# Two layers over 64 graphs on one core: attention rows divided before they are turned, and outputs in seven half-size products

## The chip, the core and the metric

The kernel runs on one core of a Trainium2 chip. The metric is device time in microseconds (us) from the first to the last instruction of an execution with what lies around it, as the median of several runs. A profiled execution has a time of its own, and its trace covers a span that is a little shorter. The engines are named as in the profile: PE (matmuls), PEld (its weight loads), DVE (VectorE), ACT (ScalarE), POOL (GpSimd) and SP (which here only issues DMAs).

## The reference

Everything is float32. There are 64 graphs of 256 nodes with 512 features each.

```python
# layer 0: x is (64, 256, 512), adj is (64, 256, 256)
h = relu(layernorm(x))
q = h @ Wq.T + bq;  k = h @ Wk.T + bk;  v = h @ Wv.T + bv
w = adj * exp(q @ k.T)
w = w / w.sum(axis=2, keepdims=True)
x = x + w @ v
# layer 1
h = relu(layernorm(x))
A = adj + I;  d = A.sum(-1) ** -0.5
x = x + (A * d[:, :, None] * d[:, None, :]) @ (h @ W1 + b1)
```

## The kernel before

Two graphs make a pair, and there are 32 pairs. The products with Wq and Wk are merged once, at the start, into one matrix, so that each pair has six stages of matmuls:

- **g** (`pm_g`): the merged matrix times the features, which gives "keys" that already hold both projections;
- **v** (`pm_v`): the values;
- **s** (`pm_s`): the scores, written with keys on the partitions and queries along the row, so that the exponentials `wT` are already turned for the next product;
- **o** (`pm_o`, line 545): weights times values;
- **l** (`pm_l`): adjacency times normed features of layer 1;
- **w** (`pm_w`): the result of l times W1.

All but o are written as block products of half-size matrices by the Strassen-Winograd scheme: seven half-size products in place of eight, with sums of blocks before (the operands called S and T) and after. One product accumulates into a PSUM bank called the chain (product 1, then 6, 7 and 4), one into a bank called rest (5, then 3), and product 2 into a bank called side. Between two products into the chain somebody has to read the bank: most often ACT copies it (tags A0, A1, U2, U3, or the tile yS in l). The stages g, v and w have 28 matmuls of 256 columns, s and l 28 of 128. A float32 matmul shows as two instructions in the profile, so 28 matmuls are 56 records.

The stage o is plain. For each of four blocks of 128 queries and each half of the 512 features it multiplies twice, over two blocks of keys, and an extra column of ones beside the values gives the row sum: 16 matmuls, 32 records. DVE takes the reciprocal of the sum (L553) and adds the scaled product to x (L555).

Other work that is named later:

- `move_quadrants` (L311): DVE turns the features in 32x32 blocks, and then ACT copies 16 strips per pair to their places in `hT`.
- `normed` (L267): ACT's layer norm with relu, four instructions per layer and pair; the statistics are L250 and L251 on DVE, followed by five small operations on POOL.
- In l and w (`convolution`), ACT copies the product l7 (L695), scales w's first product by d (L662) and copies the product l4 into b21, a part of the tile yS (L702); DVE adds (L697), and POOL makes further sums.
- L593 adds the graph bias on DVE, and L452 writes a block of the values.
- L815 and L603 to L607 prepare the adjacency on POOL.

The kernel is written with a library that puts each engine's instructions into a queue at compile time, by when they come ready in its own reckoning, and that sets the waits. `tc.issue_after(ins)` keeps instructions behind one on the same engine. The helper `in_order` keeps most matmuls in the order of the text (in s and o they are free), and other work is hung behind named readers:

```python
work = {
    "key P1": [(measure_and_weigh, p)],
    "key P6": [(second_norm, p - 1), (find_node_sums, p - 1)],
    "key C21": [(norm_features, p + 1)],
    "key C12": [(turn_blocks, p + 1), (find_key_sums, p)],
    "value P6": [(move, p + 1, 0, 4)],
    "value C11": [(find_terms, p + 1)],
}
```

In l and w of the kernel before, the order of products is l7, w1, l4, l3, w2, then the other five of w.

Of the kernel before, what the change touches and what calls it, by code (L numbers as in the profile page):

```python
# [16 lines left out]
def kernel(  # L17
# [33 lines left out]

    nc = tc.nc
    P = 128
# [15 lines left out]
    xp = ctx.enter_context(tc.tile_pool(name="xp", bufs=3))  # L69
# [7 lines left out]
    x_tiles, a_tiles, q_tiles = {}, {}, {}  # L77

# [6 lines left out]
    def load_x(p):  # L85
        x_tiles[p] = xp.tile([P, TB, D], F32, tag="x", name=f"x_{p}")
        for g in range(G):
            nc.sync.dma_start(of_graph(x_tiles[p], g), in_dram(x, p, g))

    def load_a(p):  # L90
        a_tiles[p] = ap.tile([P, TB, N], F32, tag="a", name=f"a_{p}")
        for g in range(G):
            nc.sync.dma_start(of_graph(a_tiles[p], g), in_dram(adj, p, g))
        if p == 0:
            return


        q_tiles[p] = p1.tile([P, NB, G * N // Q, Q], F32, tag="aq", name=f"aq_{p}")
        blocks = adj[G * p : G * p + G].rearrange(
            "g (j c) (kt i r) -> i c kt (g j) r", c=Q, i=NQ, r=Q  # L100
        )
        for i in range(NQ):
            nc.sync.dma_start(q_tiles[p][i * Q : (i + 1) * Q], blocks[i])
# [6 lines left out]
    w1_21 = const.tile([P, 2, HD], F32, tag="w1_21", name="w1_21")  # L110
# [13 lines left out]
    load_x(0)  # L124
    load_a(0)
    nc.sync.dma_start(wv_rows, wv.rearrange("(c p) d -> p c d", p=P))
    load_x(1)
# [6 lines left out]
    nc.sync.dma_start(b1_all, b1.partition_broadcast(P))  # L134

# [7 lines left out]
    v = const.tile([P, TB, D + 1], F32, tag="v", name="v")  # L143
    nc.gpsimd.memset(v[:, :, HD : HD + 1], 1.0)

# [6 lines left out]
    sub, add, mult = ALU.subtract, ALU.add, ALU.mult  # L152
# [17 lines left out]
    def merge_query_key():  # L170
        m21 = p1.tile([P, 2, HD], F32, tag="A1", name="m21")
        for half, dcs in ((0, (0, 1)), (1, (0, 1)), (0, (2, 3)), (1, (2, 3))):
            for dc in dcs:
                pm = ps_m.tile([P, HD], F32, tag="pm", name=f"pm_mT_{dc}_{half}")
                for oc in range(DC):
                    nc.tensor.matmul(  # L176
                        pm,
                        wk_rows[:, oc, ts(dc, P)],
                        wq_rows[:, oc, ts(half, HD)],
# [17 lines left out]
    def bias_products():  # L197
# [4 lines left out]
        g_rows, last = weighted_rows(wq_rows, bkT, "A0")  # L202
# [13 lines left out]
    def key_row(c_rows):  # L216
        pc = ps_m.tile([P, D], F32, tag="pm", name="pc_c")
        nc.tensor.matmul(pc, ones_sq, c_rows, start=True, stop=True)
        nc.scalar.copy(c_all, pc)
# [14 lines left out]
    last_sums = {}  # L234

    def inverse_root(src, plus, name):
# [3 lines left out]
        r = sm.tile([P, TB], F32, tag="ir_r", name=f"irr_{name}")  # L240
# [3 lines left out]
    def scale_offset(p, name, scale=None):  # L244

        xt = x_tiles[p]
        mv = sm.tile([P, TB, 2], F32, tag="mv", name=f"mv_{name}")
        for t in range(TB):
            st = sm.tile([P, 6], F32, tag="st", name=f"st_{name}_{t}")
            nc.vector.bn_stats(st, xt[:, t, :])  # L250
            last_sums[name] = nc.vector.bn_aggr(mv[:, t, :], st).ins  # L251
# [11 lines left out]
    def normed(p, name, rd, nb):  # L263

        h = p2.tile([P, TB, D], F32, tag="h", name=f"h_{name}")
        for t in range(TB):
            nc.scalar.activation(  # L267
                h[:, t, :],
                x_tiles[p][:, t, :],
# [4 lines left out]
        return h  # L274

    def key_terms(p, h):

        acc = sm.tile([P, TB], F32, tag="ka", name=f"ka_{p}")
        scratch = p1.tile([P, D], F32, tag="U3", name=f"hc_{p}")
        for t in range(TB):  # L280
            nc.vector.scalar_tensor_tensor(  # L281
                scratch, h[:, t, :], 1.0, c_all, mult, mult, accum_out=acc[:, t : t + 1]
            )
        ks = sm.tile([P, TB], F32, tag="ks", name=f"ks_{p}")
        nc.vector.tensor_scalar(ks, acc, s0[:, 0:1], None, add)
        return ks

    def blocks_transposed(p, h):

        hq = p1.tile([P, TB, D], F32, tag="hq", name=f"hq_{p}")  # L290
        for t in range(TB):
            nc.vector.transpose(hq[:, t, :], h[:, t, :])
        return hq

    def transposed_features(p, h):

        hT = p2.tile([P, DC, NT], F32, tag="hT", name=f"hT_{p}")
        for t in range(TB):
            pt = ps_m.tile([P, DC, P], F32, tag="pm", name=f"pt_h_{p}_{t}")
            for dc in range(DC):  # L300
                nc.tensor.transpose(pt[:, dc, :], h[:, t, ts(dc, P)], ident)  # L301
            nc.scalar.copy(hT[:, :, ts(t, P)], pt)
        return hT

    def move_quadrants(hq, hT, which):

        src = hq.rearrange("p t (dc j c) -> p j dc t c", j=NQ, c=Q)
        dst = hT.rearrange("p dc (t i c) -> p i dc t c", i=NQ, c=Q)
        for n in which:
            i, j = n // NQ, n % NQ  # L310
            last = nc.scalar.copy(dst[j * Q : (j + 1) * Q, i], src[i * Q : (i + 1) * Q, j])  # L311
        return last.ins

    def feature_sums(p, hT):

        b11, b12 = hT[:, 0:2, 0:N], hT[:, 0:2, N:NT]
        b21, b22 = hT[:, 2:4, 0:N], hT[:, 2:4, N:NT]
        hS = p2.tile([P, 3, 2, N], F32, tag="hS", name=f"hS_{p}")
        t1, t2, t4 = (hS[:, i] for i in range(3))
        eng = nc.vector if p == 0 else nc.gpsimd  # L320
        eng.tensor_tensor(t1, b12, b11, sub)
        eng.tensor_tensor(t2, b22, t1, sub)

        eng.tensor_tensor(b12, b22, b12, sub)
        eng.tensor_tensor(t4, b21, t2, sub)
        return (b11, b21, b22, t1, t2, b12, t4)

    def key_sums(p, gT):

        a11, a21 = gT[:, 0:2, 0:N], gT[:, 0:2, N:NT]  # L330
        a12, a22 = gT[:, 2:4, 0:N], gT[:, 2:4, N:NT]
        gS = p1.tile([P, 3, 2, N], F32, tag="gS", name=f"gS_{p}")
        s1, s2, s4 = (gS[:, i] for i in range(3))
        eng = nc.vector
        eng.tensor_tensor(s1, a21, a22, add)
        eng.tensor_tensor(s2, s1, a11, sub)

        eng.tensor_tensor(a21, a11, a21, sub)
        eng.tensor_tensor(s4, a12, s2, sub)
        return (a11, a12, a22, s1, s2, a21, s4)  # L340

    last_product = [None]

    def in_order(*args, **kwargs):

        with tc.issue_after(last_product[0]) if last_product[0] else ExitStack():
            last_product[0] = nc.tensor.matmul(*args, **kwargs).ins  # L347

    def products_of(name, w, weight_moves):

        banks = {}

        def product(bank, which, part, start):

            if start:
                banks[bank] = ps_m.tile([P, 2, HD], F32, tag="pm", name=f"pm_{name}_{bank}")
            for r in range(2):  # L360
                for dt in range(2):
                    left, right = w[:, which, dt, :], part[:, dt, :]
                    if weight_moves:
                        left, right = right, left
                    in_order(
                        banks[bank][:, r, :],
                        left[:, ts(r, P)],
                        right,
                        start=start and r == 0 and dt == 0,
                        stop=r == 1 and dt == 1,  # L370
                        skip_group_check=True,
                    )
            return banks[bank]

        return product

    def temp(tag, name):
        return p1.tile([P, 2, HD], F32, tag=tag, name=f"{tag}_{name}")

    def projections(p, parts, then, fill_first, fill_second):  # L380

        b11, b21, b22, t1, t2, t3, t4 = parts
        gT = p1.tile([P, DC, NT], F32, tag="gT", name=f"gT_{p}")
        keys_of = products_of(f"g_{p}", m_set, False)  # L390
        values_of = products_of(f"v_{p}", v_set, True)

        def bias(i, r):
            return gb[:, 2 * i + r : 2 * i + r + 1]

        def key_block(i, g):
            return gT[:, 2 * i : 2 * i + 2, ts(g, N)]

        def key_sum(i, g, pm, more):
            for r in range(2):  # L400
                last = nc.vector.scalar_tensor_tensor(  # L401
                    key_block(i, g)[:, r, :], pm[:, r, :], bias(i, r), more[:, r, :], add, add
                )
            return last

        def value_block(i, g):
            return v[:, 2 * g : 2 * g + 2, i * (HD + 1) : i * (HD + 1) + HD]

        def behind(ins, place):
            with tc.issue_after(ins.ins):  # L410
                then(place)

        a, u2, u3 = (temp(tag, f"g{p}") for tag in ("A1", "U2", "U3"))
        chain = keys_of(0, A11, b11, True)
        behind(nc.scalar.copy(a, chain), "key P1")  # L415
        rest = keys_of(2, S1, t1, True)
        keys_of(0, S2, t2, False)
        behind(nc.scalar.copy(u2, chain), "key P6")
        side = keys_of(1, A12, b21, True)
        behind(key_sum(0, 0, side, a), "key C11")  # L420
        keys_of(0, S3, t3, False)
        behind(nc.scalar.copy(u3, chain), "key P7")
        behind(key_sum(1, 1, rest, u3), "key C22")
# [528 lines left out]
```

## Time and profile before

| | |
|---|---|
| median of 3 runs | 1825.99 us (1825.42 to 1826.48) |
| profiled execution, own time | 1824.66 us |
| its span | 1822.9 us |
| PE / PEld / DVE / ACT / POOL busy | 99% / 90% / 70% / 47% / 51% |
| granted clock of PE | 1.0 throughout |
| DMA | 148.44 MB, 81 GB/s over the span |

Busy time is the time in which an engine has an instruction under way. PE's matmuls are pipelined and their ends are modelled, so its 99% does not say by itself that it is at its peak. A row of the groups gives line, engine, operation, tiles, shape and count, then total busy time and the mean of one in ns, and then idle time just before and who ended it. Where instructions of an engine overlap, busy time divided by the count is less than the mean of one. A row of a timeline gives start, duration, engine, line, operation and tiles, and in brackets the idle time before it and who ended that.

### The profile page before, as it was taken

Reading aid. Unit: us, or ns where it says so; the run is one execution under the profiler, and the core shown is the slowest. Engines: PE = TensorE matmul, PEld = TensorE weight load, DVE = VectorE, ACT = ScalarE, POOL = GpSimd, SP = SyncE. Lnnn points to the kernel's source line nnn. Section 1 sums busy time; section 2 is a strip of 40 time slices with the busy share of each in tenths; the row PEclk is TensorE's granted clock in tenths of the full one; section 3 lists DMA queues with packets and bytes.
Section 4 is the critical chain, followed back from the end, with each engine's and each line's share of the span. In section 5 each row is a group of like instructions: output and inputs, shape, how many; then the busy total and the mean of one; then the engine's idle time right before and its main releaser. Section 6 shows DMA issues by size and latency. Waiting matters only on the chain.

```text
span 1822.9 us, 28081 instructions
## 1 busy us (share of the span) xinstructions
PE 1810.8 (99%) x10114; PEld 1639.7 (90%) x10114; DVE 1267.9 (70%) x3030; ACT 861.3 (47%) x1604; POOL 927.5 (51%) x1099
## 2 busy tenths in 40 slices
PE   9999999999999999999999999999999999999998
PEld 8899989999999999899999999998999999999987
DVE  7867677676677676776766776767767677667664
ACT  4544554444544445544455444455444554444522
POOL 2564444655445644446554456444465544564435
PEclk9999999999999999999999999999999999999999
DMA  9444235433345342354342444423444334534111
GB/s 231 69 89 93 55 62 99 90 90 84 43 89 99 85 95 51 66 99 88 92 82 42 93 99 86 94 51 66 99 89 91 82 41 93 99 86 94 31 24 47
DMA packets 224267, 148.44 MB, mean 81 GB/s; under 512 B 150272, under 2 KB 170752, under 8 KB 224128
## 3 DMA queue, kind: packets, MB, share of 16 engines
q1 hardware_dynamic: 206112, 112.03, 28.7%
q0 software_dynamic: 16960, 33.56, 11.0%
q8 instruction: 81, 1.33, 0.4%
q10 hardware_dynamic: 1056, 1.05, 0.2%
q14 instruction: 58, 0.48, 0.1%
HBM read 112.99 MB, written 33.62 MB: 80 GB/s over the span
## 4 chain that ended last, share of the span: by engine, by line
PE 98%; POOL 1%; DVE 1%; issue 0%; ACT 0%; DVEq 0%; POOLq 0%; ACTq 0%
PE pm_g L347 21%; PE pm_v L347 21%; PE pm_w L347 21%; PE pm_o L545 12%; PE pm_s L490 11%; PE pm_l L347 11%; PE pm_mT L176 1%; PE pm_run_in L168 0%; ACT h_b L267 0%; DVE hc L281 0%; POOL x L674 0%; DVE x L668 0%; PE pt_h L301 0%; DVE ad L576 0%; PE pt_wv L226 0%
## 5 line engine op out<-in xcount | busy, mean ns | idle before, releaser
L347 PE MATMUL pm_w<-w_set,yS 128*128 128x256 f32 x1792 | 399.2, 380 | 3.2 <-DVE x L668 2.0
L347 PEld LDWEIGHTS pm_w<-w_set,yS 128*128 128x128 f32 x1792 | 335.4, 190 | 46.7 <-DVE x L668 2.6
L311 ACT COPY hT<-hq 32x512 f32<-32x512 f32 x496 | 305.4, 616 | 6.6
L698 POOL TENSOR_TENSOR yS<-yS,U_l 128x512 f32<-128x512 f32 x32 | 40.6, 1268 | 479.9 <-DVE yS L697 479.9
L347 PE MATMUL pm_v<-v_set,hT 128*128 128x256 f32 x1024 | 236.8, 379 | 0.0
L347 PE MATMUL pm_g<-hT,m_set 128*128 128x256 f32 x1024 | 236.7, 379 | 0.0
L668 DVE SCALAR_TENSOR_TENSOR x<-pm_w,irr_d,x 128x256 f32<-128x256 f32 x256 | 111.9, 479 | 166.7 <-PE pm_w L347 145.7
L545 PE MATMUL pm_o<-v,wT 128*128 128x257 f32 (+1 forms) x1024 | 227.3, 379 | 0.0
L347 PEld LDWEIGHTS pm_g<-hT,m_set 128*128 128x128 f32 x1024 | 194.7, 190 | 26.8 <-issue 0.5
L545 PEld LDWEIGHTS pm_o<-v,wT 128*128 128x128 f32 x1024 | 191.3, 189 | 26.6 <-DVE wT L511 0.3
L347 PEld LDWEIGHTS pm_v<-v_set,hT 128*128 128x128 f32 x1024 | 192.4, 190 | 24.8
L347 PE MATMUL pm_v<-v_set,hS 128*128 128x256 f32 x768 | 176.5, 380 | 0.0
L347 PE MATMUL pm_g<-hS,m_set 128*128 128x256 f32 x768 | 176.2, 379 | 0.0
L347 PEld LDWEIGHTS pm_g<-hS,m_set 128*128 128x128 f32 x768 | 146.0, 190 | 19.8
L401 DVE SCALAR_TENSOR_TENSOR gT<-pm_g,gb,U_g 128x256 f32<-128x256 f32 x128 | 56.1, 479 | 152.8 <-PE pm_g L347 111.1
L347 PEld LDWEIGHTS pm_v<-v_set,hS 128*128 128x128 f32 x768 | 143.5, 190 | 18.2
L674 POOL TENSOR_TENSOR x<-x,U_w 128x512 f32<-128x512 f32 x64 | 81.3, 1270 | 102.4 <-ACT U_w L662 99.7
L415 ACT COPY A_g<-pm_g 128x512 f32<-128x512 f32 x32 | 18.7, 585 | 235.2 <-PE pm_g L347 234.4
L555 DVE SCALAR_TENSOR_TENSOR x<-pm_o,rsum,x 128x256 f32<-128x256 f32 x256 | 110.4, 473 | 1.1
L815 POOL TENSOR_TENSOR aT<-aT,ident 128x128 f32<-128x128 f32 x128 | 65.8, 560 | 72.1 <-DVE wT L511 72.1
L347 PE MATMUL pm_l<-aT,h_b 128*128 128x128 f32 x768 | 96.3, 275 | 0.5 <-DVE U_l L689 0.5
L490 PE MATMUL pm_s<-hT,gT 128*128 128x128 f32 x768 | 96.4, 275 | 0.2
(153 smaller groups left out, 3187.4 us busy)
## 6 DMA issues: line engine op xcount, KB each, us to landing
x<-in_x_dram SPq DMA_DIRECT2D x64, 512.0 KB, 4.8
x<-in_L_gnn_Wv_b_dram POOLq DMA_DIRECT2D x32, 1024.0 KB, 11.0
out_dram<-x SPq DMA_DIRECT2D x62, 512.0 KB, 3.4
a<-in_adj_dram SPq DMA_DIRECT2D x64, 256.0 KB, 11.6
aq<-in_adj_dram SPq DMA_DIRECT2D x124, 128.0 KB, 4.4
drow<-dflat SPq DMA_DIRECT2D x32, 256.0 KB, 4.5
wq_rows<-in_L_gnn_Wq_w_dram ACTq DMA_DIRECT2D x2, 512.0 KB, 7.6
wk_rows<-in_L_gnn_Wk_w_dram SPq DMA_DIRECT2D x2, 512.0 KB, 6.8
```

Source lines behind the costliest of these rows:

```text
L176: nc.tensor.matmul(pm, wk_rows[:, oc, ts(dc, P)], wq_rows[:, oc, ts(half, HD)], start=oc == 0, stop=oc == DC - 1,)
L311: last = nc.scalar.copy(dst[j * Q : (j + 1) * Q, i], src[i * Q : (i + 1) * Q, j])
L347: last_product[0] = nc.tensor.matmul(*args, **kwargs).ins
L401: last = nc.vector.scalar_tensor_tensor(key_block(i, g)[:, r, :], pm[:, r, :], bias(i, r), more[:, r, :], add, add)
L415: behind(nc.scalar.copy(a, chain), "key P1")
L490: nc.tensor.matmul(banks[bank][:, g, :], left[:, dt, ts(g, P)], right[:, dt, ts(g, P)], start=start and g == 0 and dt == 0, stop=g == 1 an ...
L545: nc.tensor.matmul(pm[:, 0:width], wT[:, kb, qb, g, :], v[:, kb * G + g, lo : lo + width], start=kb == 0, stop=kb == NB - 1,)
L555: nc.vector.scalar_tensor_tensor(xh, pm[:, 0:HD], rsum, xh, mult, add)
L668: last = nc.vector.scalar_tensor_tensor(to, pm[:, r, :], factor(nb, r), to, mult, add)
L674: return nc.gpsimd.tensor_tensor(block(i, nb), block(i, nb), more, add)
L698: nc.gpsimd.tensor_tensor(t2, b22, part, sub)
L815: last = nc.gpsimd.tensor_tensor(diag, diag, ident, add)
```

## The change

- The roles of query and key in the merged matrix are exchanged, so that the scores stand with queries on the partitions (`e`), and the mask gives the row sums by its accumulator.
- `scale_weights` divides the rows on ACT, `turn_weights` turns them in 32x32 blocks on DVE, and `move_weights` copies 16 strips to their places in `wT` on ACT.
- The stage o becomes a seven-product scheme with sums of weights and of values on POOL, and three of its results go to x by way of ACT and POOL.
- The value tile loses its columns of ones. The features are loaded a second time into a tile of their own, in which they are normed in place; x is then loaded later into two buffers in place of three.
- All matmuls of the stages follow one list of tokens: a letter for the stage, a number for the product (1 to 7). Work hangs behind the readers of a token. In the round of pair p, the letters g, v and s belong to pair p+1, and o, l and w to pair p.

The core of the diff:

```diff
+    def scale_weights(p):
+        rs = sm.tile([P, TB], F32, tag="rsum", name=f"rsum_{p}")
+        nc.vector.reciprocal(rs, row_sums[p])
+        for t in range(TB):
+            row = weights[p][:, t // G, t % G]
+            nc.scalar.mul(row, row, rs[:, t : t + 1])
+
+    def turn_weights(p):
+        turned[p] = p1.tile([P, NB, G, NB, P], F32, tag="gS", name=f"eq_{p}")
+        for qb in range(NB):
+            nc.vector.transpose(
...
+    def move_weights(p, first, last):
+        if first == 0:
+            wTs[p] = p1.tile([P, NB, G, NB, P], F32, tag="wT", name=f"wT_{p}")
+        src = turned[p].rearrange("p qb g kb (j c) -> p j (qb g kb) c", c=Q)
+        dst = wTs[p].rearrange("p qb g kb (i c) -> p i (qb g kb) c", c=Q)
+        for n in range(first, last):
+            i, j = n // NQ, n % NQ
+            nc.scalar.copy(dst[j * Q : (j + 1) * Q, i], src[i * Q : (i + 1) * Q, j])
+
+    def find_weight_sums(p):
...
+        weight_parts[p] = left_sums(nc.gpsimd, quarters, wS)
+
+    def find_value_sums(p):
...
+        eng = nc.gpsimd if p < NP - 1 else nc.vector
+        value_parts[p] = right_sums(eng, quarters, vS)
...
-        for qb in range(NB):
-            for g in range(G):
-                t = qb * G + g
-                rsum = sm.tile([P, 1], F32, tag="rsum", name=f"rsum_{p}_{t}")
-                for half in range(2):
-                    width = HD + 1 - half
-                    lo = half * (HD + 1)
-                    pm = ps_m.tile([P, HD + 1], F32, tag="pm", name=f"pm_o_{p}_{t}_{half}")
-                    for kb in range(NB):
-                        nc.tensor.matmul(
...
-                    if half == 0:
-                        nc.vector.reciprocal(rsum, pm[:, HD : HD + 1])
-                    xh = xt[:, t, ts(half, HD)]
-                    nc.vector.scalar_tensor_tensor(xh, pm[:, 0:HD], rsum, xh, mult, add)
+    def output_stage(p):
...
+        def into(n, i, bank):
+            read(nc.vector.tensor_tensor(block(n, i), bank, block(n, i), add))
+
+        def by_way_of(tag, n, i):
+            more = temp(tag, f"o{p}")
+            read(nc.scalar.copy(more, pm["chain"]))
+            read(nc.gpsimd.tensor_tensor(block(n, i), block(n, i), more, add))
+
+        def p_1():
+            pm["chain"] = product(0, a11, b11, True)
+            by_way_of("A0", 0, 0)
...
+    def value_stage(p):
...
+        def p_7():
+            product(0, t3, S3)
+            u3 = temp("A1", f"v{p}")
+            read(nc.scalar.copy(u3, pm["chain"]))
+            read(nc.vector.tensor_tensor(block(1, 1), pm["rest"], u3, add))
+
+        def p_4():
+            product(0, t4, A22)
+            read(nc.vector.tensor_copy(block(1, 0), pm["chain"]))
...
+    def neighbour_stages(p):
...
+        def l_4():
+            gather(0, a22, u4)
+            read(nc.scalar.copy(b21, pm["l"]))
...
+        def w_2():
+            into(0, 0, product(1, b21, A12, True))
...
+    def run(order, stages, work=None):
...
+            begun[letter][number]()
+            todo = [c for c in (work or {}).get(token, ()) if c[1] < NP]
+            if todo:
+                with ExitStack() as behind:
+                    for ins in last_read.values():
+                        behind.enter_context(tc.issue_after(ins))
+                    for call, p, *more in todo:
+                        call(p, *more)
...
+    def work_around(p):
...
+            "g1": [(turn_adjacency, p), (norm_features, p + 2)],
+            "g6": [(find_weight_sums, p)],
...
+            "o3": [(measure_again, p)],
+            "v5": [(find_query_sums, p + 1)],
+            "v6": [(move, p + 2, 12, 16), (second_norm, p), (find_node_sums, p), (load_features, p + 3)],
+            "s1": [(find_terms, p + 2)],
+            "s3": [(load_a, p + 3)],
+            "l7": [(scale_weights, p + 1)],
+            "l3": [(find_feature_sums, p + 2)],
+            "w2": [(turn_weights, p + 1)],
+            "w6": [(move_weights, p + 1, 0, 6)],
+            "w5": [(measure, p + 3)],
+            "w7": [(move_weights, p + 1, 6, 16)],
+            "w3": [(find_value_sums, p + 1)],
+            "w4": [(add_graph_bias, p), (store, p), (load_x, p + 2)],
...
+    for p in range(NP - 2):
+        run(
+            "g1 g5 g6 g2 g7 o1 o5 g4 o6 g3 o2 o7 v1 o4 o3 v5 v6 v2 v7 s1 s6 v4 s5 v3 s7 "
+            "l1 s2 l2 s4 l6 s3 l5 l7 w1 l4 l3 w2 w6 w5 w7 w3 w4",
+            around(p),
+            work_around(p),
+        )
```

The work behind o6, o7 and v1 includes the other 12 strips of the features of pair p+2 (four, two and six). `read` notes an instruction as the last reader on its engine. The list above serves 30 pairs; the first pair has a list of its own, and so have the last two, in which the weights of the last pair are scaled behind s3 and moved behind v6 and v2.

## The prediction, made before the changed kernel was run

> **What bounds the kernel now.** I read the page's shares first, then its chain, then the long form of the chain, then one pair's window.
>
> ```profile
> PE 1810.8 (99%) x10114; PEld 1639.7 (90%) x10114; DVE 1267.9 (70%) x3030; ACT 861.3 (47%) x1604; POOL 927.5 (51%) x1099
> PE 98%; POOL 1%; DVE 1%; issue 0%; ACT 0%; DVEq 0%; POOLq 0%; ACTq 0%
> ```
>
> A busy share of PE alone proves little, but the chain that ended last is 98% PE: nearly every matmul waited only for the one before it. The chain in order of time repeats itself:
>
> ```profile
> 1620.42 6.93 PE pm_o L545 x32
> ...
> 1659.50 10.41 PE pm_w L347 x48
> 1669.91 6.25 PE pm_s L490 x56
> 1676.16 6.93 PE pm_o L545 x32
> ```
>
> One pair of graphs takes 1676.16 - 1620.42 = 55.74 us. A 256-column matmul instruction (a matmul is two records) costs 6.93/32 = 0.2166 us for o and 10.41/48 = 0.2169 for w; g's row 8.63/40 gives 0.2158. A 128-column one costs 6.25/56 = 0.1116. Three stages of 56 at 0.2158, two of 56 at 0.1116 and o's 32 make 36.3 + 12.5 + 6.9 = 55.7: the period is issue of matmuls and nothing else. The table of stretches agrees (columns: window, its length, then busy PE, PEld, DVE, ACT, POOL):
>
> ```profile
> 1340.00:1395.74 55.74, 55.74 (x315) 50.55 (x314) 39.09 (x94) 26.97 (x51) 28.75 (x34) 1.00 0.44 81
> ```
>
> So fewer matmuls pay one for one, and so does every wait that PE gains.
>
> [...] two of L815 took 0.88 us, and 1.18 us beside DVE's masks.
>
> **The change, part by part.**
>
> *Matmuls.* o falls from 32 instructions to 7 products x 2 graphs x 2 = 28: 6.93 - 28 x 0.2158 = 0.89 us per pair, 28.4 us in 32 pairs. The first pair's adjacency is no longer turned on PE (26.08 to 26.95 in PE's timeline): 0.9. Together **-29.3 us**. Scores by query and the new order change no count. The period would be 54.85.
>
> *Added load, per pair.* ACT: 16 pieces of the turned weights; the operation is not in the trace. Each has 256 elements per partition, so between the 0.372 of a 128x256 copy and L311's 0.616; [...] 6.4 us. Four scalings of 128x256: 0.419 each from L662 (53.6/128), at most 0.47 by interpolation in the other activations; I take 0.45: 1.8. Three copies at 0.585: 1.8. ACT goes from 27.0 to 37. POOL: three additions at 1.27, four weight sums at about 0.74 (as L603 to L607), four value sums at 1.27: 11.9, so 28.8 to 40.7. DVE: two transposes (1.3) and accumulating masks (2.0) replace masks (1.6), reciprocals (0.7) and L555 (3.5, against four 128x512 additions, 2.8): 39.1 to about 39.5. All fit under 54.85 as totals, so PE covers them unless a single wait sticks out. The second load of x adds 1 MB per pair to DMA engines busy 44%; it is issued a pair ahead and hidden. SP issues two more loads per pair, and at a pair's end the next x waits behind the store in the same buffer; POOL's addition of bv into it comes 16 us of matmuls later, against some 3.4 for a store and 4.8 for a load. Cost zero; if a load came late, POOL would hold o's sums and the second norm.
>
> *Wait A: the division in front of b21.* The list puts `scale_weights` behind l7; after it come w1, l4, l3, w2. w2 needs b21, which ACT copies from l4. The kernel before has the same four steps in the same order:
>
> ```profile
> 1377.12 1.89 PE L347 MATMUL pm_w<-w_set,yS 128*128 128x256 f32 x8
> 1377.36 0.58 ACT L695 COPY A_l<-pm_l 128x512 f32<-128x512 f32 x1 [3.96 <-PE pm_l L347]
> 1377.98 0.69 DVE L697 TENSOR_TENSOR yS<-pm_l,A_l 128x512 f32<-128x512 f32 x1 [0.24 <-ACT A_l L695]
> ...
> 1379.10 0.84 ACT L662 ACTIVATE A_w<-pm_w,irr_d 128x256 f32<-128x256 f32 x2 [1.15 <-PE pm_w L347]
> ...
> 1379.94 0.58 ACT L702 COPY yS<-pm_l 128x512 f32<-128x512 f32 x1
> ...
> 1380.57 10.23 PEld L347 LDWEIGHTS pm_w<-w_set,yS 128*128 128x128 f32 x48
> ```
>
> The copy ends at 1380.52 and the weight load starts at 1380.57: no slack. The reciprocal is queued on DVE behind the same addition as L697, so the four scalings can start at about 1378.67 + 0.17 = 1378.85, ahead of the w1 reads: ACT then runs them to 1380.65, the reads to 1381.49 and the copy to 1382.07. **PE waits 1.5 us**; if they fall between the reads and the copy, 1.75.
>
> *Wait B: the second norm in front of v7's copy.* Behind v6 stand four moves (L311, 2.5 us for four) and `second_norm` (four of L267 at 93.7/128 = 0.73: 2.9). v7's copy of the chain bank is next on ACT, and v4 adds into that bank once s1 and s6 (2 x 0.893) are out. Count from v7's end: v6's copy ends 3.45 - 0.25 - 0.58 = 2.62 before it, the moves 0.1 before it, the norms 2.8 after it, the copy 3.4 after; v4 was due at 1.79. **PE waits 1.6 us**, provided the norms are ready when the moves end. o3 ends 6.9 us before v7; its addition, what is left of four statistics at 0.66 and POOL's five small operations (2.1, as from 1350.39 on) end about 1 us before the moves do. They are ready.
>
> That an earlier block is queued whole before a later reader is seen on DVE:
>
> ```profile
> 1373.60 1.89 PE L347 MATMUL pm_v<-v_set,hT 128*128 128x256 f32 x8
> ...
> 1374.41 2.73 DVE L593 SCALAR_TENSOR_TENSOR x<-b_all,ds,x 128x512 f32<-128x512 f32 x4
> 1377.06 0.68 DVE L452 TENSOR_TENSOR v<-pm_v,A_v 128x512 f32<-128x512 f32 x1
> ```
>
> L452 reads a product that ended at 1375.33, and waited for all four of L593. Wait A costs 30 x 1.5 = 45 us, wait B 30 x 1.6 = 48; bounds for each are 0 (another queue order) and 1.75. When they exist, what waited on ACT later has slack from the same stall.
>
> *Once only.* The first pair's weights need 1.8 + 1.3 + 6.4 us of scaling, turning and moving, plus queued copies and a norm, behind v3 and five g products (10.4 us of cover): 2 to 5 us. The end loses some old stalls and gains new ones behind 16 moves. I take **+5**, bounds 0 and +10.
>
> **Sum.** Profiled execution of before 1824.66 (span 1822.9, 1.8 around it), 1.3 below the median of 1825.99. 1824.66 - 29.3 + 45 + 48 + 5 = 1893.4, and with 1.3 **1895**.
>
> **The rivals.**
> 1. *One wait only.* B disappears if the norms are queued late, A if the scalings are queued behind b21's copy. 1802 + 45 = 1847, or 1850. For it: the two orders are decided apart, and B hangs on a readiness with 1 us to spare. Against: both blocks stand ahead in program order.
> 2. *Neither (faster).* PE's list is kept and ACT's queue puts the reader first at both places. 1824.66 - 29.3 + 5 + 1.3 = 1802, 1797 without one-off costs. It decides at 0.89 us: as long as a pair's added waits stay below that, the change gains. For it: ACT has 18 us free per pair. Against: the copy with 0.05 us of slack.
> 3. *POOL becomes the bound.* 40.7 us stretched as L815 was (1.18/0.88) gives 54.6, just under PE's 54.85. It would add under 1 us per pair, near 1830 if it came alone; more likely it gives a few tenths before o5, where the weight sums end only about 1 us early. I fold it into the ranges.
>
> **How the numbers follow.** Both waits 0.42, own range 1875 to 1908; one wait 0.31 (1838 to 1862); neither 0.25 (1796 to 1810); the gain just eaten 0.02. The range must reach down to the last large case: 1797 to 1908. A difference under 0.2% (3.7 us) is about what a measurement of this kernel cannot tell from no change; so faster 0.25, same 0.02, slower 0.73.
>
> **What would show it.** The period between pairs: 54.9 for neither, 56.4 for one, 58 for both. pm_w should then list idle PE released by ACT's yS, about 45 us, and pm_v idle PE released by ACT's U or A copy, about 48. pm_o should fall to 896 records. I am wrong on A if the scalings lie after b21's copy in ACT's timeline, on B if the norms lie after v7's copy, and altogether if the period is below 55.74.

## The result, and the profile after

| | before | after |
|---|---|---|
| median | 1825.7 us (1825.37 to 1826.48, 4 runs) | 2156.73 us (2155.34 to 2158.46, 4 runs) |
| ratio to before | | 1.1813 (1.1792 to 1.1833) |
| profiled span | 1822.9 us | 2153.6 us |
| mean granted clock of PE | 1.0 | 0.952 |

The change costs 331 us. The forecast of "slower" held, but the predicted 1895 us and the upper end of its range, 1908, are far too low.

The page's shares and its chain for the changed kernel:

```profile
PE 1882.9 (87%) x9978; PEld 1672.3 (78%) x9978; DVE 1437.3 (67%) x3012; ACT 1162.6 (54%) x2338; POOL 1378.7 (64%) x1438
PE 43%; POOL 30%; ACT 12%; DVE 9%; issue 6%; DMA 0%; DVEq 0%; ACTq 0%; SPq 0%; POOLq 0%
```

Two things stand here. The chain is no longer PE's: 30% of it is POOL's. And PE is busy for 72.1 us *longer* (1882.9 against 1810.8), although it has 136 records fewer. So the 330.7 us of span are two sums: PE idle went from 12.1 us (1822.9 - 1810.8) to 270.7 (2153.6 - 1882.9), which is +258.6, and PE busy +72.1.

PE's groups say whom the idle time waits for (columns: count, then busy time and mean ns of one, then idle time just before the group and who ended it):

```profile
L497 PE MATMUL pm_w<-w_set,yS 128*128 128x256 f32 x1792 | 403.8, 383 | 33.6 <-ACT yS L851 28.9
L497 PE MATMUL pm_g<-hT,m_set 128*128 128x256 f32 x1024 | 292.2, 437 | 151.3 <-ACT U_g L568 151.3
L497 PE MATMUL pm_v<-v_set,hS 128*128 128x256 f32 x768 | 184.4, 391 | 66.7 <-ACT A_v L627 66.7
```

The first row is wait A of the prediction (w2 for b21), the third is wait B (v4 for v7's copy). The second is neither. It is the largest, and it is called **wait C** below: product g7 waits for ACT's copy of the chain bank, some 5.2 us in each of 29 pairs. The same row gives the second surprise: 437 ns for the mean matmul of g, where it was 379 in the kernel before:

```profile
L347 PE MATMUL pm_g<-hT,m_set 128*128 128x256 f32 x1024 | 236.7, 379 | 0.0
```

**Where C comes from.** The timeline at the start of one pair (start, duration, engine, line, operation, count; idle time before it and who ended that):

```profile
1124.54 0.17 DVE L268 BATCH_NORM_AGGREGATE mv_a<-st_a 128x2 f32<-128x6 f32 x1
1125.28 1.27 POOL L394 TENSOR_TENSOR vS<-v 128x512 f32<-128x512 f32 x1
...
1127.01 0.59 ACT L561 COPY A_g<-pm_g 128x512 f32<-128x512 f32 x1 [0.19 <-PE pm_g L497]
1128.19 1.71 POOL L396 TENSOR_TENSOR v<-v 128x512 f32<-128x512 f32 x1
1129.99 0.56 POOL L257 TENSOR_SCALAR irs_a<-mv_a 128x4 f32<-128x4 f32 x1
...
1132.40 1.03 POOL L259 TENSOR_TENSOR irr_a<-irs_a,minus_half 128x4 f32<-128x4 f32 x1
...
1133.52 0.20 POOL L277 TENSOR_TENSOR nb_a<-nm_a,irr_a 128x4 f32<-128x4 f32 x1
...
1133.75 2.93 ACT L283 ACTIVATE h_a<-h_a,nb_a,irr_a 128x512 f32<-128x512 f32 x4 [6.16 <-POOL nb_a L277]
...
1136.59 0.56 ACT L568 COPY U_g<-pm_g 128x512 f32<-128x512 f32 x1
1137.30 3.49 PE L497 MATMUL pm_g<-hT,m_set 128*128 128x256 f32 x8 [5.20 <-ACT U_g L568]
```

Read it from the bottom. g7 waits 5.2 us for the copy L568. The copy stands in ACT's queue behind the first norm of pair p+2, which the list hangs behind g1. That norm waits 6.16 us with nothing before it but an empty engine, until POOL has written `nb_a`. The statistics were finished at 1124.7. But POOL works on the value sums of the next pair (L394 to L397), which the list puts behind w3, and its small operations, which need about 2 us, get through only by 1133.7. No engine has too much work in all: ACT stands idle here, and POOL, which is busy almost throughout this stretch, is busy for 64% of the span. Two queues hold the wrong thing at their head.

**Where the longer busy time comes from.** The table of stretches around the same gap (length, then busy PE, PEld, DVE, ACT, POOL, then PE's granted clock, DMA share and GB/s):

```profile
1125.03:1132.00 6.97, 6.97 (x33) 5.89 (x31) 6.82 (x9) 2.33 (x6) 6.73 (x7) 1.00 0.09 33
1132.00:1137.30 5.30, 0.10 (x2) 0.04 (x1) 1.09 (x3) 3.40 (x5) 5.14 (x9) 0.97 0.78 222
1137.30:1140.60 3.30, 3.30 (x8) 2.68 (x9) 0.00 (x0) 0.00 (x0) 3.14 (x7) 0.53 1.17 327
1125.03:1192.10 67.07, 58.78 (x310) 52.32 (x309) 44.20 (x94) 36.31 (x74) 43.47 (x46) 0.95 0.37 83
```

Behind the gap of 5.2 us eight records take 3.30 us, which is 0.41 each instead of 0.216, at a granted clock of 0.53; ahead of the gap the clock is 1.00. In all 29 pairs that have this gap, the clock of the first 1.80 us behind it is 0.50. Experiment 5 asks whether the gap lowers it. The last row is the whole pair: it takes 67.07 us, and PE is busy for 58.78 of them; before, a pair took 55.74.

### The profile page after: what moved, and what is told of

It reads as the page before. It is cut to its first block, busy times and chain, and to the rows that moved or that the text cites. A ratio compares the mean times of both kernels' runs of the same rounds, so it can differ in the third digit from the quotient of the medians.

```text
span 2153.6 us, 29007 instructions
## 1 busy us (share of the span) xinstructions
PE 1882.9 (87%) x9978; PEld 1672.3 (78%) x9978; DVE 1437.3 (67%) x3012; ACT 1162.6 (54%) x2338; POOL 1378.7 (64%) x1438
## 4 chain that ended last, share of the span: by engine, by line
PE 43%; POOL 30%; ACT 12%; DVE 9%; issue 6%; DMA 0%; DVEq 0%; ACTq 0%; SPq 0%; POOLq 0%
PE pm_g L497 10%; PE pm_o L497 9%; PE pm_v L497 9%; PE pm_s L497 7%; PE pm_l L497 7%; POOL x L824 5%; DVE st_b L267 4%; ACT h_b L283 3%; ACT h_a L283 3%; ACT e L419 2%; POOL v L396 2%; POOL vS L395 2%; POOL irr_b L259 2%; POOL yS L857 2%; POOL hS L397 2%
## 5 line engine op out<-in xcount | busy, mean ns | idle before, releaser
L497 PE MATMUL pm_w<-w_set,yS 128*128 128x256 f32 x1792 | 403.8, 383 | 33.6 <-ACT yS L851 28.9
L497 PE MATMUL pm_g<-hT,m_set 128*128 128x256 f32 x1024 | 292.2, 437 | 151.3 <-ACT U_g L568 151.3
L497 PEld LDWEIGHTS pm_g<-hT,m_set 128*128 128x128 f32 x1024 | 223.3, 222 | 199.1 <-POOL aT L467 161.8
L497 PE MATMUL pm_v<-v_set,hS 128*128 128x256 f32 x768 | 184.4, 391 | 66.7 <-ACT A_v L627 66.7
L497 PE MATMUL pm_v<-v_set,hT 128*128 128x256 f32 x1024 | 241.7, 384 | 0.0
L554 DVE SCALAR_TENSOR_TENSOR gT<-pm_g,gb,U_g 128x256 f32<-128x256 f32 x128 | 58.0, 479 | 252.0 <-ACT U_g L575 248.3
L847 POOL TENSOR_TENSOR yS<-yS,U_l 128x512 f32<-128x512 f32 x32 | 40.7, 1271 | 271.4 <-DVE rsum L416 262.1
L438 ACT COPY wT<-eq 32x256 f32<-32x256 f32 x512 | 205.6, 402 | 7.3 <-DVE eq L425 1.3
L283 ACT ACTIVATE h_a<-h_a,nb_a,irr_a 128x512 f32<-128x512 f32 x128 | 93.8, 803 | 184.4 <-POOL nb_a L277 184.4
L339 DVE SCALAR_TENSOR_TENSOR x<-b_all,ds,x 128x512 f32<-128x512 f32 x128 | 161.0, 1315 | 0.0
L349 DVE SCALAR_TENSOR_TENSOR hc<-h_a,c_all 128x512 f32<-128x512 f32 x128 | 156.1, 1220 | 1.1
L739 POOL TENSOR_TENSOR x<-x,A_o 128x512 f32<-128x512 f32 x64 | 83.3, 1303 | 112.5 <-ACT A_o L738 103.6
L828 ACT COPY yS<-pm_l 128x512 f32<-128x512 f32 x32 | 18.7, 586 | 206.0 <-PE pm_l L497 206.0
L823 ACT ACTIVATE U_w<-pm_w,irr_d 128x256 f32<-128x256 f32 x128 | 53.8, 471 | 137.9 <-PE pm_w L497 137.9
L666 ACT ACTIVATE e<-e,ks 128x128 f32<-128x128 f32 x192 | 66.6, 394 | 90.7 <-DVE e L710 48.4
```

Source lines behind the costliest of these rows:

```text
L283: nc.scalar.activation(h[:, t, :], xt[:, t, :], AF.Relu, bias=nb[:, t : t + 1], scale=rd[:, t : t + 1],)
L339: nc.vector.scalar_tensor_tensor(xt[:, t, :], b1_all, ds[p][:, t : t + 1], xt[:, t, :], mult, add)
L349: nc.vector.scalar_tensor_tensor(scratch, feats[p][:, t, :], 1.0, c_all, mult, mult, accum_out=acc[:, t : t + 1])
L554: nc.vector.scalar_tensor_tensor(block(i, n)[:, r, :], bank[:, r, :], bias(i, r), more[:, r, :], add, add)
L666: nc.scalar.activation(block(qb, kb)[:, g], scores[:, g], AF.Exp, bias=terms[p][:, t : t + 1])
L739: read(nc.gpsimd.tensor_tensor(block(n, i), block(n, i), more, add))
```

## The experiments

The first four ask one question of each wait: move its cause, and see what is left.

**1. Wait C, from POOL's side.** The value sums are kept behind `nb_a` on POOL (`last_small` holds the instruction that writes it); ACT's order stays.

```diff
...
-        value_parts[p] = right_sums(eng, quarters, vS)
+        with tc.issue_after(last_small[f'a{p + 2}']) if p < NP - 2 else ExitStack():
+            value_parts[p] = right_sums(eng, quarters, vS)
```

> In the changed kernel, the value sums on POOL are issued behind the five small operations that follow the statistics of pair p+3's features (so that nb_a comes first); nothing else moves. Theory 1 (one chain: POOL's value sums stand ahead of nb_a, ACT's first norm waits for nb_a, the copy of g6 waits behind that norm, and g7 waits for the copy): the idle time ahead of g7, 151 us in the trace, goes, and with it the half-speed matmuls after it (8 records in 3.32 us where 1.73 is normal, 1.6 us in each of 30 pairs, 48 us): 2156.7 - 151 - 48 = about 1958 us. Rival (POOL has too much work in all, 43.7 us of the 66.5 us period, and a new order only moves its lateness to the o products, which need the value sums): at most a quarter of that comes back, 2105 us or more, and pm_o lists the idle time.

Measured: 2002.26 us, ratio 1.0972 (1.0953 to 1.0990). The groups of PE in this kernel (its line 500 is line 497 of the changed one):

```profile
L500 PE MATMUL pm_g<-hT,m_set 128*128 128x256 f32 x1024 | 236.7, 379 | 0.0
L500 PE MATMUL pm_v<-v_set,hS 128*128 128x256 f32 x768 | 210.3, 431 | 97.1 <-ACT A_v L630 97.1
```

C is gone whole, and g is back at 379 ns. So it is POOL's value sums, ahead of the small operations, that cause it. Of the 199 us expected, 154 came. Most of the rest turned up at B, whose idle grew from 66.7 to 97.1 us, and whose slow matmuls grew too (184.4 to 210.3). ACT's timeline of this kernel shows how (the moves ahead of this norm ended at 1132.61):

```profile
1134.44 2.93 ACT L285 ACTIVATE h_b<-x,nb_b,rs_b 128x512 f32<-128x512 f32 x4 [1.83 <-POOL nb_b L279]
```

ACT now waits 1.83 us for `nb_b`, where it was 0.78. In this kernel DVE ends the statistics 1.4 us before the moves end, and in the changed one 2.5 (1156.15 against 1158.61): with PE no longer stopped at g7, DVE's and POOL's work on the second norm comes later against ACT's. The long stop had covered part of the short one.

**2. Wait C, from ACT's side.** The norm moves from g1 to o1, the turning behind o6, the strips behind o7, v1, v6 and s6; POOL's order stays.

```diff
-            "g1": [(turn_adjacency, p), (norm_features, p + 2)],
+            "g1": [(turn_adjacency, p)],
...
-            "g7": [(turn_blocks, p + 2)],
...
+            "o1": [(norm_features, p + 2)],
...
```

> In the changed kernel, ACT's first norm of pair p+2 is queued behind o1 in place of g1, with the turning of its blocks behind o6 and the 16 strips behind o7, v1, v6 and s6; POOL's order stays. Theory 1 (the norm stands at the head of ACT's queue and waits, so the reader behind it is late): PE's idle time ahead of g7 goes although nb_a is as late as before: about 1958 us. Rival (PE waits at g7 for POOL itself, whose late sums the trace names for pm_g's weight load): no more than 50 us comes back, above 2105 us.

Measured: 1968.47 us (1961.27 to 1977.13), ratio 1.0787 (1.0754 to 1.0820). The same group of PE in this kernel:

```profile
L497 PE MATMUL pm_g<-hT,m_set 128*128 128x256 f32 x1024 | 236.9, 379 | 0.3 <-ACT U_g L568 0.3
```

So both links are needed: break the one on POOL or the one on ACT, and C goes. B grew here as well, to 79.8 us.

**3. Wait B alone.** The second norm, its sums and the load of the features go from v6 to v7, so that v7's copy stands in front of them.

```diff
-            "v6": [(move, p + 2, 12, 16), (second_norm, p), (find_node_sums, p), (load_features, p + 3)],
+            "v6": [(move, p + 2, 12, 16)],
+            "v7": [(second_norm, p), (find_node_sums, p), (load_features, p + 3)],
```

> In the changed kernel, the second norm (with the sums and the load that hang on it) is queued behind v7 in place of v6. Theory (wait B of the prediction, and the slower clock that follows it): pm_v's 67 us of idle time go, and the slow records after it (in one pair 2.20, 1.71 and 2.20 us for v4, s5 and v3 where 1.73, 0.89 and 1.73 are normal: 1.76 us, times 30 is 53): 2156.7 - 120 = about 2037 us. Rival (only the idle time counts, the slow records have another cause such as DMA traffic): about 2090 us. Second rival (l1 then waits for the norm instead): within 30 us of 2157.

Measured: 2076.78 us, ratio 1.1377 (1.1360 to 1.1394). PE's groups:

```profile
L497 PE MATMUL pm_g<-hT,m_set 128*128 128x256 f32 x1024 | 292.2, 437 | 151.6 <-ACT U_g L568 151.6
L497 PE MATMUL pm_v<-v_set,hS 128*128 128x256 f32 x768 | 177.0, 380 | 2.5 <-ACT A_v L627 2.5
```

B is gone but for 2.5 us at the end of the kernel, and C is untouched. The idle part came as expected (66.7 to 2.5). The clock part did not: PE's busy time fell by only 13.6 us (1882.9 to 1869.3), where 53 were expected. The expectation had taken the 1.76 us of one slow pair thirty times. In the changed kernel's PE timeline v4 is slow behind this gap in nine pairs (2.41 to 2.82 us for its eight records; granted clock 0.78 to 0.90 in its first 1.80 us) and takes 1.99 in the other 21, at a clock of 1.00; nine times 1.76 is 16. Most of the lost clock hangs on C: g keeps its 437 ns.

**4. Wait A alone.** `scale_weights` goes from l7 to l3, behind the copy into b21.

```diff
-            "l7": [(scale_weights, p + 1)],
-            "l3": [(find_feature_sums, p + 2)],
+            "l3": [(scale_weights, p + 1), (find_feature_sums, p + 2)],
```

> In the changed kernel, the division of the rows on ACT is queued behind l3 in place of l7, that is behind the copy into b21. Theory (wait A of the prediction, 0.96 us in each of 30 pairs, too short for the clock to fall): about 2124 us. Rival (turning and moving the weights then come too late, and o1 waits for them): 2157 us or more.

Measured: 2112.59 us, ratio 1.1576 (1.1558 to 1.1593). Two of PE's groups:

```profile
L497 PE MATMUL pm_w<-w_set,yS 128*128 128x256 f32 x1792 | 401.9, 382 | 4.8 <-POOL yS L857 4.5 <-DVE yS L855 0.2
L497 PE MATMUL pm_g<-hT,m_set 128*128 128x256 f32 x1024 | 295.7, 441 | 160.9 <-ACT U_g L568 160.9
```

All 28.9 us for ACT's `yS` are gone from the idle time of pm_w (what is left is POOL's sums at the kernel's end). But 44 us came back where 33 were expected, and of the 40.8 by which the profiled spans differ these are the smaller part. C grew by 9.6 us (151.3 to 160.9), so that PE's idle time as a whole fell by only 18.7 (270.7 to 252.0). The other 22.1 are busy time (1882.9 to 1860.8). Most of that is the clock behind B, for 13.2 of it stands in the groups that hold v4, s5 and v3 (184.4 to 182.2, 75.0 to 67.9 and 241.7 to 237.8): v4, whose gap is still 2.14 us, now runs at full clock in 29 of 30 pairs. The last section comes back to this. As expected, A costs no clock: behind its gaps of 0.96 us the changed kernel has a granted clock of 1.00 in all 30 pairs.

**5. The clock.** Eleven more matmuls of 256 columns stand ahead of g7 in 30 pairs and keep PE busy in the gap. That is 660 more records, so 142.4 us more work at 0.2158.

```diff
+            if 0 < p < NP - 1:
...
+                for n in range(11):
+                    in_order(spare, m_set[:, A11, 0, 0:P], b11[:, 0, :], start=True, stop=True)
             product(0, S3, t3)
```

> In the changed kernel, 11 matmuls of 256 columns into a bank that nobody reads are put ahead of g7 in 30 pairs (22 records, 4.7 us, inside the idle stretch of 5.2 us); they compute nothing that is used. Theory (the granted clock falls because PE is idle, so g7's eight records take 3.32 us in place of 1.73): these records return to 1.73 and the kernel is up to 48 us faster though it does more work, about 2110 us. Rival (the DMA burst of that moment, 222 to 327 GB/s, slows the operands' reads): no change, 2157 us; or slower where the idle stretch is shorter than the added work.

Measured: 2112.14 us, ratio 1.1575 (1.1558 to 1.1593): 45 us faster with more to do. PE's timeline, at g7 and at v4 of one pair:

```profile
1112.60 1.96 PE L497 MATMUL pm_g<-hT,m_set 128*128 128x256 f32 x8 [0.45 <-ACT U_g L568]
...
1136.62 3.63 PE L497 MATMUL pm_v<-v_set,hS 128*128 128x256 f32 x8 [2.14 <-ACT A_v L631]
```

The table of stretches of the same kernel, for g7 and for v4:

```profile
1112.60:1114.40 1.80, 1.80 (x8) 1.60 (x9) 0.00 (x0) 0.00 (x0) 1.65 (x4) 1.00 1.05 405
1136.62:1140.09 3.47, 3.47 (x9) 2.81 (x10) 3.06 (x6) 0.21 (x1) 3.39 (x3) 0.52 0.03 5
```

Eight records of g7 take 1.96 us here, where they took 3.49. The loads run beside them as fast as ever (405 GB/s), and the clock is 1.00. In the pair shown v4 has next to no loads beside it (5 GB/s), a clock of 0.52, and takes 3.63. So the rival, that the burst of loads slows PE, is out. PE's busy time without the added records is 1979.5 - 142.4 = 1837.1, 45.8 below the changed kernel's: most of g7's share of the loss. Not all is cured: v4's group rose from 184.4 to 204.5 us, for it is slow in 16 pairs now, where it was slow in nine. Keeping PE busy in one gap moved part of the price to the next.

**6 to 8. All three waits at once**: C by POOL's side (edits 4, 3 and 1), C by ACT's side (edits 4, 3 and 2), and both.

> The three edits together: value sums on POOL behind nb_a, second norm behind v7, division behind l3. Theory (three waits through ACT's queue and the slow clock behind them are the whole loss): idle time 151, 67 and 29 us and the 101 us by which PE's busy time stands above 1781 go: about 1809 us, faster than the kernel before by 0.9%. Rival (POOL, with about 44 us of work in a period of 55 and longer operations beside DVE, shows up as a fourth wait, at o5 or at w7): 1840 to 1900 us.

> The first norm behind o1 (ACT's side of the first wait), second norm behind v7, division behind l3. Theory as for all_pool: about 1809 us. Rival: the four strips behind s6 and the norms behind v7 crowd the scores' exponentials, and s7 or l1 waits: 1830 to 1880 us.

> all_pool and all_act together, so both the order on POOL and the order on ACT. Theory: no fourth wait is left that either would have taken away; within 5 us of the faster of the two, about 1805 us. Rival: value sums behind nb_a reach o5 too late (its value sum t1 is then ready about 1 us ahead of it): 10 to 30 us slower than all_act.

Measured: 1823.98 us, ratio 0.9993 (0.9985 to 1.0002); 1828.48 us, ratio 1.0018 (1.0010 to 1.0026); and with both 1822.25 us, ratio 0.9983 (0.9975 to 0.9990). So the 331 us are these three waits and the clock that they cost, and nothing else of that size. But none reaches the time expected. The last one's shares, and one of its pairs:

```profile
PE 1792.6 (98%) x9978; PEld 1617.0 (89%) x9978; DVE 1356.5 (75%) x3012; ACT 1170.0 (64%) x2338; POOL 1357.7 (75%) x1438
...
1005.83:1060.79 54.96, 54.96 (x309) 49.73 (x308) 41.47 (x95) 36.62 (x74) 42.71 (x46) 1.00 0.44 101
```

In the middle no wait is left: PE is busy for 54.96 of 54.96 us at full clock, 0.78 us below the 55.74 of before, and it is busy without a gap from 120 to 1700 us of the span. PE's timeline has its gaps at the ends:

```profile
71.97 2.08 PE L500 MATMUL pm_o<-v,wT 128*128 128x256 f32 x4 [4.30 <-ACT wT L440]
78.67 2.07 PE L500 MATMUL pm_o<-vS,wS 128*128 128x256 f32 x4 [4.62 <-POOL wS L386]
...
1788.36 8.02 PE L500 MATMUL pm_w<-w_set,yS 128*128 128x256 f32 x24 [4.49 <-POOL yS L860]
```

The first pair has to scale, turn and move its weights with little beside it, and then to sum them on POOL behind the value sums. The last round does the same for the last pair among the norms.

**9. The ends mended.** In the first pair g4 and g3 come ahead of o1, and its value sums go to DVE. In the last round half of the strips go from v2 to v7, the adjacency sums from O4 to l3.

```diff
-        eng = nc.gpsimd if p < NP - 1 else nc.vector
+        eng = nc.gpsimd if 0 < p < NP - 1 else nc.vector
...
+            ("g1 g5 g6 g2 g7 g4 g3 o1 o5 o6 o2 o7 " if p == 0 else
...
```

> The kernel is the one with all three waits taken away (1822.25 us), with its once-only places mended too: the first pair multiplies g4 and g3 ahead of o1 and makes its value sums on DVE, and in the last round the second half of the last weights' strips is moved behind v7 instead of v2, and the last adjacency sums lie behind l3 instead of O4. Theory (what is left over the prediction's unhindered 1802 stands at the two ends, once): the 4.3 and 4.6 us in front of o1 and o6, the 2.5 in front of v4 and the 4.5 in front of the last rows of w go, with some 3 to 5 us of slow clock behind them: 1804 to 1810, ratio to before 0.989 to 0.992. Rival (the rest is a little in every pair, spread too thin to be seen as a wait): 1818 to 1823.

Measured: 1817.17 us (1816.70 to 1818.05), ratio 0.9952 (0.9939 to 0.9966). It is the fastest of all and beats the kernel before by 0.5%, but gains 5.1 us where 12 to 18 were expected. PE's timeline of this kernel:

```profile
72.72 3.78 PE L500 MATMUL pm_g<-hS,m_set 128*128 128x256 f32 x8 [4.92 <-ACT U_g L578]
```

The two waits ahead of o1 and o6 (4.30 and 4.62) are gone, and one of 4.92 stands a few products earlier: the sixteen strips, 6.6 us of ACT, now stand in front of g7's copy. In the last round v4 still waits 2.48 for ACT, and the 4.49 in front of w has become 1.08 and 2.41.

**10. The ends once more.** Ten of the strips go behind g7, the statistics of the last round behind o3, its norms behind s2 and w6, the sums behind w5, the last strips behind v7 and l1. The graph biases of the last two pairs, which were behind w5 and w4, both go behind w4.

```diff
-            "v3": [(measure, 2), (move_weights, 0, 0, 16), (find_value_sums, 0)],
+            "v3": [(measure, 2), (move_weights, 0, 0, 6), (find_value_sums, 0)],
...
+            "g7": [(move_weights, p, 6, 16), (find_weight_sums, p)] if p == 0 else [],
...
-            "s3": [(second_norm, p), (scale_weights, p + 1)],
+            "s2": [(second_norm, p)],
+            "s3": [(scale_weights, p + 1)],
...
```

> The kernel with both ends mended (1817.17 us), with the waits that its trace still shows there attacked once more: ten of the first pair's sixteen strips come behind g7 (all sixteen stood in front of g7's copy, 4.9 us), and in the last round the statistics come behind o3 and the norm behind s2 (norm and scalings stood in front of v7's copy, 2.5 us), the strips behind v7 and l1, and the last pair's norm and node sums behind w6 and w5 (1.1 and 2.4 us in front of w7 and w3). Theory: about 8 us of these 10.9 go, and 1 to 3 us of slow clock behind them: 1806 to 1810. Rival (each of these blocks of work is too long for any place at the ends, and stands in front of the next reader): 1813 to 1818.

Measured: 1819.45 us, ratio 0.9970 (0.9958 to 0.9982), so no gain over experiment 9. PE's timeline, and DVE's near the end:

```profile
73.52 1.99 PE L500 MATMUL pm_g<-hT,m_set 128*128 128x256 f32 x8 [3.41 <-DVE gT L557]
...
1788.75 5.38 DVE L341 SCALAR_TENSOR_TENSOR x<-b_all,ds,x 128x512 f32<-128x512 f32 x8
1794.83 0.69 DVE L840 TENSOR_TENSOR U_l<-pm_l,yS 128x512 f32<-128x512 f32 x1
...
1795.67 2.04 PE L500 MATMUL pm_l<-aT,h_b 128*128 128x128 f32 x8 [6.93 <-DVE U_l L840]
```

The rival describes it, and the time even lies just above the rival's range. The wait of 4.92 has shrunk, but g3 now waits for DVE, which makes the value sums first. The statistics behind o3 hold up the scores (2.76 us), v4 still waits for the division (2.92 us), and l waits 6.93 us for an addition that stands on DVE behind the node sums and all eight graph biases (5.38 us). At the ends too little other work lies beside these blocks. That what is left there can't be had at all is not shown; a third order was not tried.

## Why the prediction was wrong, step by step

**The direction, slower: right.** It is not luck that it held: with C gone the kernel is still slower than before (1968 and 2002 us), by A, B and their clock.

**Matmuls, -29.3 us: right.** pm_o has 896 records (384 + 256 + 128 + 128). Where no wait stands, a pair takes 54.96 us; 54.85 was predicted.

**Added load: right.** A strip took 205.6/512 = 0.402 us (6.4/16 = 0.40 predicted; before's copies give that estimate too, 0.372 + (0.616 - 0.585) = 0.403), a scaling 54.6/128 = 0.427 (0.45). Without the waits ACT has 36.6 us of a pair (37), POOL 42.7 (40.7), DVE 41.5 (39.5). Every total fits under 54.96. The second load of x costs PE nothing per pair (busy for 54.96 of 54.96 us in experiment 8, at a DMA share of 0.44).

**Wait A, +45: right in place and mechanism, too large.** It is 28.9 us, 0.96 per pair in place of 1.5. That work queued earlier on ACT holds up a later reader was the author's assumption; the prediction shows it on DVE alone. Here l4 ended at 1112.70, and its copy L851 started at 1113.94, behind the scalings and the reads; with the scalings queued behind that copy (experiment 4) the 28.9 us are gone. ACT's timeline runs in the predicted order:

```profile
1110.12 0.59 ACT L845 COPY A_l<-pm_l 128x512 f32<-128x512 f32 x1 [0.25 <-PE pm_l L497]
1111.61 1.71 ACT L419 ACTIVATE e<-e,rsum 128x256 f32<-128x256 f32 x4 [0.90 <-DVE rsum L416]
1113.22 0.82 ACT L823 ACTIVATE A_w<-pm_w,irr_d 128x256 f32<-128x256 f32 x2
1113.94 0.57 ACT L851 COPY yS<-pm_l 128x512 f32<-128x512 f32 x1
1114.56 10.63 PE L497 MATMUL pm_w<-w_set,yS 128*128 128x256 f32 x48 [0.96 <-ACT yS L851]
```

The scalings start 1.49 us after L845, exactly as predicted. The term that was mis-sized is ACT's chain behind them. The copy ends 4.39 us after L845's start, and 4.71 were predicted: four scalings take 1.71 instead of 1.8, and neighbours overlap, so that the two reads cost 0.72 (1113.22 to 1113.94) instead of 0.84. I had summed durations where starts count. That is the whole difference, for the other 0.2 us is a matter of counting. In the kernel before, w2 starts at

```profile
1380.63 10.57 PE L347 MATMUL pm_w<-w_set,yS 128*128 128x256 f32 x48
```

which is 3.27 us after the copy L695 (1377.36). Here it starts 4.44 us after L845, so a pair loses 1.17 us. The trace counts 0.96 of them as idle, because the last matmul before a gap counts as busy to its modelled end.

**Wait B, +48: right in place and mechanism, too small.** It is 66.7 us, of which 2.5 belong to the end; that leaves 2.14 per pair, above the bound of 1.75. The step that failed is "they are ready". POOL's timeline:

```profile
1156.15 0.63 POOL L257 TENSOR_SCALAR irs_b<-mv_b 128x4 f32<-128x4 f32 x1 [2.86 <-DVE mv_b L268]
...
1157.36 1.44 POOL L259 TENSOR_TENSOR irr_b<-irs_b,minus_half 128x4 f32<-128x4 f32 x1
...
1159.15 0.20 POOL L277 TENSOR_TENSOR nb_b<-nm_b,rs_b 128x4 f32<-128x4 f32 x1
```

The five small operations took 3.2 us, beside DVE's sums for the scores, where before's trace had 2.1. They end after the moves, not 1 us ahead of them, and ACT waits 0.78 for `nb_b`.

**Wait C: missed, 151.3 us of idle.** Rival 3 looked at POOL by its total, priced a full POOL at under 1 us per pair, and expected a few tenths at the weight sums. The total was right and said nothing. The step that failed is "all fit under 54.85 as totals, so PE covers them unless a single wait sticks out", followed by a search on ACT's queue alone. What the list shows, and what I did not do, is to write POOL's queue out from w5 to g6: `measure` for the next round behind w5, value sums behind w3, the norm behind g1, and g7 as the fifth product of the round. Value sums of 5.1 us by my own price, then 2.1 of small operations, 2.9 of norm and 0.6 of copy end 10.7 us after g1's start; g7 is due after four products, at 6.9. That is a wait of 3.8 us per pair, against 151.3/29 = 5.2 measured, and the prediction had all these durations.

**The clock: missed, some 75 us.** Each wait was priced as idle time, and what follows a wait at nothing. But 1810.8 - 29.3 is 1781.5 us of matmuls at full clock, and 1882.9 were measured, 101 more. Of these, 11 are still there in experiment 8 (1792.6). Of the other 90 some 15 are no slow clock, by an estimate: at 89 gaps the last matmul counts as busy for 0.16 us (0.379 - 0.216) after the next could have started. Experiment 5 shows for g7, where most of the remaining 75 lie, that this is the granted clock. Before's trace, which the prediction went by, could not show it: from 125 to 1700 us PE is busy for 1574.96 of 1575 us at a clock of 1.00, and behind the longest wait near its end, 1.97 us ahead of w at 1795.02, the clock is 1.00 as well.

**Once only, +5 (bounds 0 and +10): too small.** With all three waits gone the kernel takes 1822.25 us, against 1802 for the case "neither". The period explains 3 of the 20 (0.11 x 30), the ends the rest, as PE has no gap between 120 and 1700 us. I had counted one late block at the start; there are two, the end has two more, and slow clock follows (0.89 from 72 to 125 us in experiment 8, where the kernel before has 1.00).

**The chances.** Each case (both, one, neither) treated waits A and B as the only places. The range took in the bounds of known waits and left no room for one in a queue that had not been looked at.

## What to carry to other kernels

Put moved or added work into the queue of every engine that issues it, in the stretch where it lands, and follow what stands behind it: a total per pair that fits says nothing about the head of a queue. A chain of two queues (POOL's sums in front of a small operation, and ACT's norm, waiting for that, in front of a copy) can stop PE while every engine has time to spare (C: 151.3 us, with POOL busy for 64% of the span and ACT for 54%). Price a gap in PE at its idle time plus what the matmuls behind it lose to a lower clock: here about 1.9 us behind each gap of C, which is 5.2 us long ((292.2 - 236.7)/29), 1.76 in one of the nine pairs in which B's 2.14 us had it, and nothing behind A's 0.96. Expect a wait that is removed to be given back in part at another one; in three of the four single edits it was (B from 66.7 us to 97.1 and to 79.8, C from 151.3 to 160.9).

## What the hardware showed that was not expected

A gap of 2.14 us was followed by eight records at half clock (v4 in experiment 5: 3.63 us at 0.52, where 1.99 is the time at full clock).

The same gap does not always cost the same. Behind gaps of 2.13 to 2.22 us v4 is slow in nine of 30 pairs of the changed kernel, in 16 of experiment 5 and in one of experiment 4. Experiment 1, whose gap at v4 is 3.18 to 3.21 us, has a pattern. Six pairs in a row:

```profile
162.37 3.40 PE L500 MATMUL pm_v<-v_set,hS 128*128 128x256 f32 x8 [3.19 <-ACT A_v L630]
223.55 3.15 PE L500 MATMUL pm_v<-v_set,hS 128*128 128x256 f32 x8 [3.19 <-ACT A_v L630]
284.74 2.90 PE L500 MATMUL pm_v<-v_set,hS 128*128 128x256 f32 x8 [3.20 <-ACT A_v L630]
345.89 2.62 PE L500 MATMUL pm_v<-v_set,hS 128*128 128x256 f32 x8 [3.18 <-ACT A_v L630]
407.07 1.99 PE L500 MATMUL pm_v<-v_set,hS 128*128 128x256 f32 x8 [3.21 <-ACT A_v L630]
466.57 3.67 PE L500 MATMUL pm_v<-v_set,hS 128*128 128x256 f32 x8 [3.18 <-ACT A_v L630]
```

The time falls by about 0.25 us from pair to pair until v4 runs at full clock, and then it starts again from the top. The granted clock over these six is 0.57, 0.62, 0.67, 0.75, 1.00 and 0.51. While v4 is slow the pairs stand 61.15 to 61.19 us apart; from the pair at full clock to the next it is 59.50. So the length of a gap alone does not give what it costs: behind 3.18 to 3.21 us v4 took between 1.99 and 3.67. What else decides it is not shown; no run was made to test that.

POOL and DVE took longer beside each other. The graph bias on DVE (L339) took 1315 ns beside POOL's value sums; before it was 768, and with the sums elsewhere in experiment 8 it is 786 (its line 341). The sums took up to 1.71 us in place of 1.27, which made C longer (the four took 5.84 us in the pair shown, where four at 1.27 are 5.08).
